# One pool of eight slots for the mixer's and FFN's short-lived tiles, and transfers that the scheduler counts in one line

## The chip, the cores and the metric

The kernel runs on one core of a Trainium2 chip. The time is the device time of one launch in microseconds (us). The kernel before takes 4589.91 us, the median of three runs (4589.24 to 4595.37).

## The reference, cut to what matters

Thirty-two images of 96 channels and 56 x 56 pixels pass through two layers. The first is a convolution block with 576 inner channels. The second works on the 3136 pixels as tokens: a mixer that goes through a Fourier transform over the tokens, and a feed-forward part (FFN) whose numbers are rounded to small float formats.

```python
# layer 0: convolution block, per image
h = relu(bn1(einsum('oc,bchw->bohw', w1, x)))          # 96 -> 576
h = relu(bndw(depthwise_conv3x3(h, wdw)))
x = x + bn2(einsum('oc,bchw->bohw', w2, h))            # 576 -> 96
# layer 1: on tokens t [image, 3136, 96]
h = relu(bn1(einsum('bnc,hc->bnh', layernorm(t), w1)))  # 96 -> 192
X = fft(h, axis=1, norm='ortho')
xr = relu(X.real * rd - X.imag * idg + rb)
xi = relu(X.imag * rd + X.real * idg + ib)
t = t + bn2(einsum('bnh,ch->bnc', ifft(xr + 1j * xi, axis=1, norm='ortho').real, w2))
u = layernorm(t)
h = relu(qlinear(u, W1, b1))                            # 96 -> 384, rounded
t = t + qlinear(h, W2, b2)
# ... (batch norms have stored statistics; qlinear rounds inputs, sums and biases)
```

## The kernel before

The kernel is written as a list of steps. Each step has an engine, an estimated cost, the steps it comes after, the buffers that it takes and gives back, a rank (which of the ready steps is preferred), and `late`, the time from the end of its work until its result counts as there. While the program is built, `Plan.emit` plays these steps through with the estimated times and writes the instructions in the order that comes out. On the chip each engine then works through its own list in that order and waits on semaphores where a result isn't there. The guesses are used at no other place: a wrong one does not change the result, it changes the order.

```python
START = {"last": 9, "front": 7, "mid": 62, "back": 98}     # offsets of rank for the stages
PACE = {"last": 3.023, "front": 0.4, "mid": 0.54, "back": 0.45}
OFF = (-4.5, 0.5, 0.5, 8.0)
AT = (3.0, 0.5)

class Plan:
    LATE = {"PE": 0.3, "ACT": 0.18, "DVE": 0.15}
    def moved(self, now, moves):                # `late` of a transfer
        size, rate, extra = moves
        start = now + 1.4
        end = start + size / rate
        self.moving = [m for m in self.moving if m[1] > start - 20]
        wait = sum(max(0.0, min(end, b) - max(start, a)) for a, b in self.moving)
        self.moving.append((start, start + 1.3 * size / rate))
        return end + wait + extra - now
    def emit(self):
        # ... of the ready steps of an idle engine, in order of rank:
                    short = {b for b in s.take if self.free[b] < s.take.count(b)}
                    if short or wanted.intersection(s.take):
                        wanted |= short
                        passed.append(item)
                        continue
        # ... and, when it is taken:
                    late = self.moved(now, s.late) if isinstance(s.late, tuple) else s.late
                    heapq.heappush(events, (now + cost, count, engine, None))
                    heapq.heappush(events, (now + cost + late, count + 1, None, s))

def read(n):    return n * 4, 170e3, 1.5        # a load: bytes, bytes per us, extra us
def written(n): return n * 4, 170e3, 3.0        # a write to memory
```

Four stages make an image. In the convolution, `unit` works on half an image and 128 of the inner channels. ACT makes a product of one tap in a tile of its own, and a transfer from GpSimd's queue adds it into `acc`; then ACT applies the ReLU to `acc`.

```python
nc.scalar.activation(acc[img, s, k], u["hs"][...], AF.Identity, scale=..., bias=...)        # line 643
nc.scalar.activation(u["p", dr][...], u["hs"][...], AF.Copy, scale=weight(dr, 0))          # line 659
nc.vector.scalar_tensor_tensor(dst, src, weight(dr, dc), dst, ALU.mult, ALU.add)           # line 670
nc.gpsimd.dma_start(out=t[...], in_=u["p", dr][...], accum_op=ALU.add)                     # line 678
nc.scalar.activation(acc[img, s, k], acc[img, s, k], AF.Relu)                              # line 687
# ... the transfer's step, with W = 28 * 56:
t = step("POOL", 1.0, add(None, 0), [t] + c, [], ["product"], late=(W * 128 * 4, 200e3, 0.0), rank=4 * n + 3)
```

`front` projects to 96 channels, keeps the tokens in memory (`tdr`), takes the norm, and sends the first transform's result to memory (`ydr`). `mid` reads it back and has three parts per half image, each with a tile V, a tile eo and a tile sb:

```python
u["V", part] = w2.tile([128, G, 2, S], F32, name="V")                        # pool of 2
u["eo", part] = w1.tile([128, G, 2, S], F32, name="eo", bufs=3)              # pool of 3
to = u["b", part] = w1.tile([128, G, SK], F32, name="sb", tag="brief", bufs=3)   # pool of 3
# ... t = step("PE", cost, spread(part), need, ["ps", "V", "eo", "brief"], ...)
# ... t = step("DVE", 2 * dve(392, 0.1), fold(part), [t], [], ["V", "brief"])
# ... t0 = step("PE", ..., half_project, folds, ["ps", "ps"], ["eo"]), and project(t) gives the other eo
```

Lines 1135 and 1136 (ACT) and 1152 (DVE) work on V and sb, lines 1167 and 1170 (DVE) fold them into eo. The pool `brief` of three holds sb, and also xn (the scaled tokens, line 979), pj and gc (results of the projection and of the inverse transform, lines 1235 and 1263) and o (the output, line 1463). `back` reads the mixer's result from memory (`gdr`), takes the norm (line 837 its square root on ACT, line 853 the reciprocal on DVE), and computes the FFN (lines 1350 to 1463).

Of the kernel before, what the change touches and what calls it, by code (L numbers as in the profile page):

```python
# [32 lines left out]
F32 = mybir.dt.float32  # L33
# [8 lines left out]
C = 96  # L42
HD = 576
S = 56
# [3 lines left out]
SK = 2 * S  # L48
# [7 lines left out]
G = 7  # L56
# [72 lines left out]
PACE = {"last": 3.023, "front": 0.4, "mid": 0.54, "back": 0.45}  # L129
CHAIN = 0.6  # L130

SPARSE = 0.75
FILLER = 0.23
FIRST = 15.0
# [20 lines left out]
class Plan:  # L155
# [12 lines left out]
    def __init__(self, free):  # L168
        self.free = dict(free)
        self.steps = []  # L170
        self.now = self.pace = 0.0
        self.window, self.share, self.slow = 0, {}, False
        self.moving = []
        self.filler, self.recent = None, []

    def stretched(self, now, work):
# [22 lines left out]

    def moved(self, now, moves):  # L200

        size, rate, extra = moves
        start = now + 1.4
        end = start + size / rate
        self.moving = [m for m in self.moving if m[1] > start - 20]
        wait = sum(max(0.0, min(end, b) - max(start, a)) for a, b in self.moving)
        self.moving.append((start, start + 1.3 * size / rate))
        return end + wait + extra - now

    def job(self, now, pace):  # L210

# [2 lines left out]
    def step(self, engine, cost, emit, after=(), take=(), give=(), late=None, rank=None):  # L214
        late = self.LATE.get(engine, 0.1) if late is None else late
        if rank is None:
            rank = self.now
            self.now += self.pace
        s = Step(engine, cost, emit, list(after), list(take), list(give), late, rank, len(self.steps))
        self.steps.append(s)  # L220
        return s
# [62 lines left out]
def tile_kernel(ctx: ExitStack, tc: tile.TileContext, d: dict, out: bass.AP):  # L284
# [66 lines left out]
    hl = [cst([128, RP + 1, S], f"hl{s}") for s in range(2)]  # L351


    scratch = [w1.tile([128, G * SK], F32, name="eo", bufs=3) for _ in range(3)]
    scratch += [w2.tile([128, G * SK], F32, name="V") for _ in range(2)]
    scratch.append(w1.tile([SK, 2 * G * SK], F32, name="wb"))
    scratch += [w2.tile([SK, G * HA], F32, name="yb") for _ in range(2)]
    used = [0] * len(scratch)
# [170 lines left out]
    def ffn():  # L529
# [6 lines left out]
        for o, v, p, n in ((b1q, fb, 128, 3), (b2q, fc, C, 1)):  # L536
# [9 lines left out]
    plan = Plan(  # L546
        {
# [4 lines left out]
        }  # L552
    )
# [9 lines left out]
        return fixed + n / 960  # L563

    def read(n):
        return n * 4, 170e3, 1.5

    def written(n):
        return n * 4, 170e3, 3.0

    bands_set = [step("DVE", 1.2, bands(j), rank=2.0 + j) for j in range(2)]
    sets = []
    for n, (f, count) in enumerate(((second, 7), (attention, 6), (mixer, 21), (ffn, 4))):
        t = step("SP", 0.55 * count, fetch, sets[-1:], late=(150e3, 170e3, 1.5), rank=-20.0 + n)
        sets.append(step("DVE", 3.0, f, sets[-1:] + [t], rank=14.0 + 4 * n))
    second_set, mixer_set, *mid_set = sets

# [22 lines left out]
    def unit(img, s, k):  # L600
# [96 lines left out]
            last = q == rest[-1]  # L697
            t = step("DVE", dve(W - 28, 0.16), tap(*q), [t] + c * last, [], ["hs"] * last, rank=4 * n + OFF[2] + at * 3.5 / len(rest))
        if k in DOUBLE:
            c = [step("POOL", 1.0, add(0, -up), c, [], ["product"], late=(W * 128 * 4, 200e3, 0.0), rank=4 * n + AT[1])]  # L700
        t = step("POOL", 1.0, add(None, 0), [t] + c, [], ["product"], late=(W * 128 * 4, 200e3, 0.0), rank=4 * n + 3)
        ready[img, s, k] = step("ACT", act(W, 0, 0.09), finish, [t], rank=4 * n + OFF[3])

    def last_channels(img, s):
# [265 lines left out]
    def mixer_in(img, s, j, v, after):  # L970
# [4 lines left out]
        def scale():  # L975

            at = slice(G * j, G * j + G)
            u["xn"] = w1.tile([SK, G, C], F32, name="xn", tag="brief", bufs=3)
            nc.vector.tensor_mul(u["xn"], v["t"][:, at, :], v["r"][:, at].unsqueeze(2).to_broadcast([SK, G, C]))

        t = step("DVE", dve(G * C, 0.06), scale, after + [sent[img, s]] * j + [mixer_set], ["brief"], ["norma", "xt"] * j)
# [90 lines left out]
    def mid(img, half):  # L1072
# [36 lines left out]
        def spread(part):  # L1109


            def f():
                u["V", part] = w2.tile([128, G, 2, S], F32, name="V")
                u["eo", part] = w1.tile([128, G, 2, S], F32, name="eo", bufs=3)
                u["X", part] = psum()
                pv = slots(u["X", part])
                for q in range(G):
                    for s in range(2) if part == 2 else (part,):
                        if part == 2:
                            o, lhsT = pv[64 * s : 64 * s + 64, q, 0:SK], u["yb", s][:, q, 128:HA]  # L1120
                        else:
                            o, lhsT = pv[:, q, 0:SK], u["yb", s][:, q, 0:128]
                        nc.tensor.matmul(o, lhsT=lhsT, rhs=u["wb"][:, G * s + q, :], start=True, stop=True)  # L1123

            return f
# [18 lines left out]
        def combine(part, op):  # L1144
            def f():
                rd = cw[:, part // 2, 0:1]
                X = slots(u["X", part])[:, 0:G, 0:SK]
                V = u["V", part].rearrange("p q r w -> p q (r w)")
                to = V
                if op == ALU.subtract:  # L1150
                    to = u["b", part] = w1.tile([128, G, SK], F32, name="sb", tag="brief", bufs=3)
                nc.vector.scalar_tensor_tensor(to, X, rd, V, ALU.mult, op)  # L1152

            return f
# [29 lines left out]
        for part in (0, 2, 1):  # L1184
            r = real and part != 1
            need = [w] + (yb if part == 2 else [yb[part]])
            cost = pe(SK, 128, 2 * G)
            t = step(
                "PE",
                cost,  # L1190
                spread(part),
                need,
                ["ps", "V", "eo", "brief"],
                ([YB] if part == 2 else []) + ([YB, WB] if part == 1 else []),
            )
            t = step("ACT", 2 * act(392, 2) + 0.24 * r, weigh(part), [t])
            t = step("DVE", dve(784), combine(part, ALU.subtract), [t])
            t = step("DVE", dve(784), combine(part, ALU.add), [t], [], ["ps"])
            t = step("ACT", act(784, 0, 0.09), bend(part), [t])
            t = step("DVE", 2 * dve(392, 0.1), fold(part), [t], [], ["V", "brief"])  # L1200
            folds.append(step("DVE", 0.08, place(part), [t]) if r else t)

        def half_project():
# [27 lines left out]

        def projected(t):
            def f():
                u["p", t] = w1.tile([SK, G * C], F32, name="pj", tag="brief", bufs=3)
                nc.scalar.activation(
                    u["p", t].rearrange("p (q c) -> p q c", c=C), slots(u["P", t])[0:SK, 0:G, 0:C], AF.Copy
                )

            return f
# [16 lines left out]
        def inverted(t):  # L1256
            def f():
                if (img, "g") not in sent:

                    gdr[img] = dram.tile([NP, SK, C], F32, name="gdr", bufs=3)  # L1260
                    sent[img, "g"] = True
                u["g", t] = w1.tile([SK, G * C], F32, name="gc", tag="brief", bufs=3)
                nc.scalar.activation(
                    u["g", t].rearrange("p (j w) -> p j w", j=2), u["I", t][0:SK, :, 0:n], AF.Copy
                )

            return f
# [9 lines left out]
            return f  # L1277

        turns.setdefault(img, [])
        t0 = step("PE", pe(C, SK, 2 * G) + 0.1, half_project, folds, ["ps", "ps"], ["eo"])  # L1280
        for t in range(2):
            p = step("PE", pe(C, SK, 2 * G), project(t), [t0], ["brief"], ["eo"])
            p = step("ACT", act(G * C), projected(t), [p], [], ["ps"])
            take = ["ps", "brief"] + ["gdr"] * (half == 0 and t == 0)
            p = step("PE", pe(n, SK, 4), invert(t), [p] + turns[img], take, ["brief"])
            turns[img] = [p]
            p = step("ACT", act(G * C), inverted(t), [p], [], ["ps"])
            sent[img, "g", half, t] = step("SP", 0.2, send(t), [p], [], ["brief"], late=written(SK * G * C))


    def back(img, h):
# [148 lines left out]
            nc.vector.tensor_scalar_add(u["y"], u["y"], b2q)  # L1440

        def total():
            u["o"] = w1.tile([C, G, SK], F32, name="o", tag="brief", bufs=3)
            u["ps"] = psum()
            pv = slots(u["ps"])
            for q in range(G):
                nc.tensor.matmul(
                    pv[0:C, q, 0:SK],
                    lhsT=u["t"][:, q, :],
                    rhs=ident[0:SK, 0:SK],  # L1450
                    start=(q in (0, 4)),
                    stop=False,
                    is_transpose=True,
                    skip_group_check=True,
                )
            yv = u["y"].rearrange("p (q w) -> p q w", w=SK)
            for a, b in HALVES:
                nc.tensor.matmul(
                    pv[0:C, a:b, 0:SK], lhsT=ident16, rhs=yv[:, a:b, :], start=False, stop=True, skip_group_check=True
                )  # L1460
# [98 lines left out]
```

## Time and profile before

| | us |
|---|---|
| time, median of 3 | 4589.91 |
| span of the profiled execution | 4584.2 |
| PE matmul busy | 4405.4 |
| VectorE (DVE) busy | 4330.6 |
| ScalarE (ACT) busy | 4114.5 |
| accumulations into acc: issue to landing, median of 256 | 8.0 |
| accumulations into another product: the same, median of 128 | 10.1 |

The profile is that of one execution. A busy share near 100% doesn't say that an engine bounds the kernel: [...] a filler matmul (line 1491) is put in wherever the plan sees PE idle for long. The lists of waits give, for an engine and a line, the line that it waited for, then the total, the times and the longest. A wait that several semaphores could have caused is put down to the one that came last. A timeline gives start, duration, engine, line, operation, and in brackets the idle time before it with what ended it.

### The profile page before, as it was taken

The page shows a single profiled execution, that of the slowest core. Times are in us where ns is not written, and L with a number is a line of the kernel's source. Part 1 is how long each engine was busy: PE and PEld are TensorE (multiplying, and loading weights), DVE is VectorE, ACT ScalarE, POOL GpSimd, SP SyncE. Part 2 cuts the span into 40 slices and gives each one's busy share as a digit, 9 for nine tenths or more (in the row PEclk, how much of TensorE's full clock was granted, in tenths as well). Part 3 has the DMA queues.
Part 4 walks back from the last instruction along what each step waited for, and adds up shares of the span by engine and source line. Part 5 has one row for each costly group of instructions (what it writes and reads, how often), then busy time and mean ns, then how long its engine had stood idle before and what let it go on. Part 6 is the DMA issues. An engine that isn't in the chain of part 4 may idle for free.

```text
span 4584.2 us, 88412 instructions
## 1 busy us (share of the span) xinstructions
PE 4405.4 (96%) x35128; PEld 3296.1 (72%) x35128; DVE 4330.6 (94%) x7053; ACT 4114.5 (90%) x5390; POOL 340.7 (7%) x403
## 2 busy tenths in 40 slices
PE   8989999999999999999999999999999999999998
PEld 5667776777777777777777777777777777777777
DVE  8998999999999999999999999999999999999967
ACT  5677999999999999999999999999999999999965
POOL 1000000000000000000000000000000000000000
PEclk9999999999999999999999999999999999999999
DMA  4666777767767777767777767777767777767663
GB/s 104 135 155 157 190 171 176 187 162 185 181 163 188 174 179 185 184 166 191 173 176 185 183 163 188 174 176 183 187 162 188 174 174 190 179 165 191 168 170 107
DMA packets 390993, 789.44 MB, mean 172 GB/s; under 512 B 135696, under 2 KB 236628, under 8 KB 390580
## 3 DMA queue, kind: packets, MB, share of 16 engines
q1 hardware_dynamic: 335028, 479.15, 36.2%
q0 software_dynamic: 55488, 304.64, 34.4%
q8 instruction: 276, 4.52, 0.4%
q14 instruction: 137, 1.12, 0.1%
q10 hardware_dynamic: 64, 0.01, 0.0%
HBM read 286.38 MB, written 192.68 MB: 105 GB/s over the span
## 4 chain that ended last, share of the span: by engine, by line
PE 48%; ACT 22%; DVE 16%; DMA 8%; issue 4%; POOLq 0%; ACTq 0%; POOL 0%; SPq 0%; DVEq 0%
PE pw L883 11%; DVE acc L670 10%; PE ps L617 9%; DMA acc<-product 7%; PE ps L1005 4%; PE ps L1123 4%; PE ps L755 3%; PE ps L1036 3%; ACT product L659 3%; ACT hs L627 2%; ACT acc L687 2%; ACT acc L643 2%; PE ps L1329 2%; ACT h L1410 2%; ACT h L1395 2%
## 5 line engine op out<-in xcount | busy, mean ns | idle before, releaser
L670 DVE SCALAR_TENSOR_TENSOR acc<-hs,wdw,acc 128x1540 f32<-128x1540 f32 (+2 forms) x1664 | 2970.3, 1792 | 26.6 <-ACT acc L643 20.8
L617 PE MATMUL ps<-xs,w1T 96*128 96x406 f32 x2048 | 819.8, 523 | 24.6 <-ACT h L1395 16.7
L883 PEld LDWEIGHTS pw<-w2T,acc 128*112 128x112 f32 x7168 | 754.3, 178 | 62.1 <-issue 36.4
L883 PE MATMUL pw<-w2T,acc 128*112 128x96 f32 x7168 | 790.8, 264 | 4.5 <-ACT acc L687 4.5
L659 ACT ACTIVATE product<-hs,wdw 128x1568 f32<-128x1568 f32 (+1 forms) x384 | 613.8, 1599 | 21.6 <-DMA product<-product 20.9
L617 PEld LDWEIGHTS ps<-xs,w1T 96*128 96x128 f32 x2048 | 368.2, 194 | 261.7 <-issue 174.0
L627 ACT ACTIVATE hs<-ps,b 128x812 f32<-128x812 f32 x512 | 481.5, 941 | 51.2 <-PE ps L617 46.8
L687 ACT ACTIVATE acc<-acc 128x1568 f32<-128x1568 f32 x256 | 387.5, 1514 | 90.9 <-DMA acc<-product 85.1
L678 POOL DMA_DIRECT2D acc<-product x256 | 222.7, 870 | 3193.9 <-DVE mf L859 781.6
L643 ACT ACTIVATE acc<-hs,bd,wdw 128x1568 f32<-128x1568 f32 x256 | 437.0, 1707 | 0.3
L755 PE MATMUL ps<-hl,band 128*64 128x385 f32 (+3 forms) x3072 | 416.1, 495 | 0.3 <-ACT hs L627 0.3
L1005 PE MATMUL ps<-watt,xnT 97*120 97x192 f32 x1792 | 345.3, 337 | 60.9 <-DVE V L1152 59.6
L1005 PEld LDWEIGHTS ps<-watt,xnT 97*120 97x120 f32 x1792 | 299.0, 187 | 125.3 <-DVE V L1152 65.6
L1123 PEld LDWEIGHTS ps<-wb,yb 112*128 112x128 f32 x3528 | 297.3, 164 | 66.5 <-issue 20.9
L1395 ACT ACTIVATE h<-ps 128x784 f16<-128x784 f32 x384 | 319.6, 835 | 25.8 <-PE ps L1383 22.0
L1350 ACT ACTIVATE u<-tt,mf,rf 112x96 fp8e5<-112x96 f32 x812 | 312.3, 460 | 16.6 <-DVE mf L859 16.5
L1123 PE MATMUL ps<-wb,yb 112*128 112x112 f32 x3528 | 321.8, 271 | 4.4 <-ACT hs L627 2.6
L1410 ACT ACTIVATE h<-h 128x784 fp8e5<-128x784 f16 x348 | 301.9, 867 | 14.9 <-DVE h L1401 14.8
L755 PEld LDWEIGHTS ps<-hl,band 128*64 128x64 f32 (+1 forms) x3072 | 151.9, 134 | 198.9 <-issue 164.2
L1152 DVE SCALAR_TENSOR_TENSOR sb<-ps,cw,V 128x784 f32<-128x784 f32 x192 | 197.0, 1026 | 31.1 <-ACT V L1136 25.4
L1018 ACT ACTIVATE z<-ps 120x768 f32<-120x768 f32 (+1 forms) x256 | 182.3, 725 | 44.9 <-PE ps L1005 44.9
L1036 PE MATMUL ps<-z,wa 56*64 56x384 f32 (+1 forms) x2048 | 217.5, 496 | 0.3
(171 smaller groups left out, 6663.3 us busy)
## 6 DMA issues: line engine op xcount, KB each, us to landing
acc<-product POOLq DMA_DIRECT2D x256, 784.0 KB, 8.0
product<-product POOLq DMA_DIRECT2D x128, 756.0 KB, 10.1
yb<-ydr SPq DMA_DIRECT2D x252, 294.0 KB
wd<-in_wd_dram SPq DMA_DIRECT2D x128, 349.1 KB
wb<-in_wb_dram SPq DMA_DIRECT2D x63, 686.0 KB
ydr<-ya SPq DMA_DIRECT2D x256, 168.0 KB
xs<-in_x_dram SPq DMA_DIRECT2D x64, 609.0 KB
tdr<-xt SPq DMA_DIRECT2D x64, 588.0 KB
```

Source lines behind the costliest of these rows:

```text
L617: nc.tensor.matmul(u[h][:, j, 0:QW], lhsT=w1T[:, 128 * k : 128 * (k + 1)], rhs=xs[img, s][0:C, at : at + QW], start=True, stop=True,)
L627: nc.scalar.activation(flat[:, 2 * h * QW : 2 * (h + 1) * QW].rearrange("p (j w) -> p j w", j=2), u[h][:, :, 0:QW], AF.Relu, bias=b1[:, k ...
L643: nc.scalar.activation(acc[img, s, k], u["hs"][:, o + up : o + up + R, :], AF.Identity, scale=weight(up, 0), bias=bd[:, k : k + 1],)
L659: nc.scalar.activation(u["p", dr][:, ra:rb, :], u["hs"][:, ra + o + dr : rb + o + dr, :], AF.Copy, scale=weight(dr, 0))
L670: nc.vector.scalar_tensor_tensor(dst, src, weight(dr, dc), dst, ALU.mult, ALU.add)
L687: nc.scalar.activation(acc[img, s, k], acc[img, s, k], AF.Relu)
L755: nc.tensor.matmul(pv[:, :, ca:cb], lhsT=band[rows, j, dc + 1, 64 * o : 64 * o + 64], rhs=H[rows, q : q + 7, ca + dc : cb + dc], skip_grou ...
L883: nc.tensor.matmul(u["pw"][0:SK, t, n % 4, 0:C], lhsT=src[rows, (G * t + n) * SK : (G * t + n + 1) * SK], rhs=rhs, skip_group_check=True, **k,
L1005: nc.tensor.matmul(pv[0:PK, q - a, 0:HA], lhsT=xnT[:, q, 0:PK], rhs=watt, start=True, stop=True,)
L1123: nc.tensor.matmul(o, lhsT=lhsT, rhs=u["wb"][:, G * s + q, :], start=True, stop=True)
L1395: nc.scalar.activation(u["h", c].rearrange("p (j w) -> p j w", j=2), u["H", c][:, :, 0:n], AF.Copy)
L1410: nc.scalar.activation(u["h8"][:, c, :], u["h", c], AF.Copy, saturate=False)
```

## The change

The tiles V and eo go into the pool `brief`, which grows from three slots to eight; 2 + 3 + 3 slots become 8 of the same size, so that any of the three kinds may have more than its share for a while. And the scheduler no longer gives each transfer its own rate with an addition for overlapping ones: all transfers stand in one line that drains at 225,000 bytes per us, with an extra of 0.5 us for loads and writes and of 1.3 us for accumulations.

```diff
+RATE = 225e3
+HARD = 0.5
+SOFT = 1.3
...
-        self.moving = []
+        self.moving = 0.0
...
-        size, rate, extra = moves
-        start = now + 1.4
-        end = start + size / rate
-        self.moving = [m for m in self.moving if m[1] > start - 20]
-        wait = sum(max(0.0, min(end, b) - max(start, a)) for a, b in self.moving)
-        self.moving.append((start, start + 1.3 * size / rate))
-        return end + wait + extra - now
+        size, extra = moves
+        self.moving = max(self.moving, now + 1.0) + size / RATE
+        return self.moving + extra - now
...
-            "xt": 1, "norma": 2, "brief": 3, "xnT": 1, "z": 2, "ya": 1, "wb": 1, "yb": 2,
-            "V": 2, "eo": 3, "real": 1, "wd": 1, "gd": 1, "tt": 2, "normf": 2, "u8": 1, "uT": 1,
+            "xt": 1, "norma": 2, "brief": 8, "xnT": 1, "z": 2, "ya": 1, "wb": 1, "yb": 2,
+            "real": 1, "wd": 1, "gd": 1, "tt": 2, "normf": 2, "u8": 1, "uT": 1,
...
     def read(n):
-        return n * 4, 170e3, 1.5
+        return n * 4, HARD
     def written(n):
-        return n * 4, 170e3, 3.0
+        return n * 4, HARD
...
-        t = step("POOL", 1.0, add(None, 0), [t] + c, [], ["product"], late=(W * 128 * 4, 200e3, 0.0), rank=4 * n + 3)
+        t = step("POOL", 1.0, add(None, 0), [t] + c, [], ["product"], late=(W * 128 * 4, SOFT), rank=4 * n + 3)
...
-                u["V", part] = w2.tile([128, G, 2, S], F32, name="V")
-                u["eo", part] = w1.tile([128, G, 2, S], F32, name="eo", bufs=3)
+                u["V", part] = w1.tile([128, G, 2, S], F32, name="V", tag="brief", bufs=8)
+                u["eo", part] = w1.tile([128, G, 2, S], F32, name="eo", tag="brief", bufs=8)
...
-                ["ps", "V", "eo", "brief"],
+                ["ps", "brief", "brief", "brief"],
```

The lines cut away change the same names in the same way: `bufs=3` becomes `bufs=8` for xn, sb, pj, gc and o, and every step that gave back V or eo gives back a `brief`.

More of the change, by code (lines that the diff above doesn't have):

```diff
@@ L351, in tile_kernel @@
     hl = [cst([128, RP + 1, S], f"hl{s}") for s in range(2)]
-    scratch = [w1.tile([128, G * SK], F32, name="eo", bufs=3) for _ in range(3)]
-    scratch += [w2.tile([128, G * SK], F32, name="V") for _ in range(2)]
+    scratch = [w1.tile([128, G * SK], F32, name="eo", tag="brief", bufs=8) for _ in range(3)]
+    scratch += [w1.tile([128, G * SK], F32, name="V", tag="brief", bufs=8) for _ in range(2)]
     scratch.append(w1.tile([SK, 2 * G * SK], F32, name="wb"))
@@ L573, in tile_kernel @@
     for n, (f, count) in enumerate(((second, 7), (attention, 6), (mixer, 21), (ffn, 4))):
-        t = step("SP", 0.55 * count, fetch, sets[-1:], late=(150e3, 170e3, 1.5), rank=-20.0 + n)
+        t = step("SP", 0.55 * count, fetch, sets[-1:], late=(150e3, HARD), rank=-20.0 + n)
         sets.append(step("DVE", 3.0, f, sets[-1:] + [t], rank=14.0 + 4 * n))
@@ L699, in unit @@
         if k in DOUBLE:
-            c = [step("POOL", 1.0, add(0, -up), c, [], ["product"], late=(W * 128 * 4, 200e3, 0.0), rank=4 * n + AT[1])]
-        t = step("POOL", 1.0, add(None, 0), [t] + c, [], ["product"], late=(W * 128 * 4, 200e3, 0.0), rank=4 * n + 3)
+            c = [step("POOL", 1.0, add(0, -up), c, [], ["product"], late=(W * 128 * 4, SOFT), rank=4 * n + AT[1])]
+        t = step("POOL", 1.0, add(None, 0), [t] + c, [], ["product"], late=(W * 128 * 4, SOFT), rank=4 * n + 3)
         ready[img, s, k] = step("ACT", act(W, 0, 0.09), finish, [t], rank=4 * n + OFF[3])
@@ L977, in scale @@
             at = slice(G * j, G * j + G)
-            u["xn"] = w1.tile([SK, G, C], F32, name="xn", tag="brief", bufs=3)
+            u["xn"] = w1.tile([SK, G, C], F32, name="xn", tag="brief", bufs=8)
             nc.vector.tensor_mul(u["xn"], v["t"][:, at, :], v["r"][:, at].unsqueeze(2).to_broadcast([SK, G, C]))
@@ L1150, in f @@
                 if op == ALU.subtract:
-                    to = u["b", part] = w1.tile([128, G, SK], F32, name="sb", tag="brief", bufs=3)
+                    to = u["b", part] = w1.tile([128, G, SK], F32, name="sb", tag="brief", bufs=8)
                 nc.vector.scalar_tensor_tensor(to, X, rd, V, ALU.mult, op)
@@ L1199, in mid @@
             t = step("ACT", act(784, 0, 0.09), bend(part), [t])
-            t = step("DVE", 2 * dve(392, 0.1), fold(part), [t], [], ["V", "brief"])
+            t = step("DVE", 2 * dve(392, 0.1), fold(part), [t], [], ["brief", "brief"])
             folds.append(step("DVE", 0.08, place(part), [t]) if r else t)
@@ L1233, in f @@
             def f():
-                u["p", t] = w1.tile([SK, G * C], F32, name="pj", tag="brief", bufs=3)
+                u["p", t] = w1.tile([SK, G * C], F32, name="pj", tag="brief", bufs=8)
                 nc.scalar.activation(
@@ L1261, in f @@
                     sent[img, "g"] = True
-                u["g", t] = w1.tile([SK, G * C], F32, name="gc", tag="brief", bufs=3)
+                u["g", t] = w1.tile([SK, G * C], F32, name="gc", tag="brief", bufs=8)
                 nc.scalar.activation(
@@ L1279, in mid @@
         turns.setdefault(img, [])
-        t0 = step("PE", pe(C, SK, 2 * G) + 0.1, half_project, folds, ["ps", "ps"], ["eo"])
+        t0 = step("PE", pe(C, SK, 2 * G) + 0.1, half_project, folds, ["ps", "ps"], ["brief"])
         for t in range(2):
-            p = step("PE", pe(C, SK, 2 * G), project(t), [t0], ["brief"], ["eo"])
+            p = step("PE", pe(C, SK, 2 * G), project(t), [t0], ["brief"], ["brief"])
             p = step("ACT", act(G * C), projected(t), [p], [], ["ps"])
@@ L1442, in total @@
         def total():
-            u["o"] = w1.tile([C, G, SK], F32, name="o", tag="brief", bufs=3)
+            u["o"] = w1.tile([C, G, SK], F32, name="o", tag="brief", bufs=8)
             u["ps"] = psum()
```

## The prediction

> **What bounds the kernel now.** I read the page first: the busy shares, the forty slices, the chain that ended last. Then the windows by stage, the waits of each engine in the steady part, and the timeline of one image.
>
> ```profile
> PE 4405.4 (96%) x35128; PEld 3296.1 (72%) x35128; DVE 4330.6 (94%) x7053; ACT 4114.5 (90%) x5390; POOL 340.7 (7%) x403
> ...
> PE 48%; ACT 22%; DVE 16%; DMA 8%; issue 4%; POOLq 0%; ACTq 0%; POOL 0%; SPq 0%; DVEq 0%
> ```
>
> Three engines are nearly full at once. PE's 96% holds matmuls that only keep its clock up (the row of line 1491: 710 in the steady part, 118.2 us), so PE has a little to give; DVE has no such filling. The chain passes through the accumulating transfers for about 8% of the span.
>
> ```profile
> 2026.64:2164.24 137.60, 133.82 (x1070) 99.41 (x1070) 132.43 (x215) 130.00 (x172) 10.46 (x12) 0.99 0.73 178
> 2164.24:2302.62 138.38, 135.30 (x1083) 100.51 (x1082) 133.88 (x215) 130.14 (x173) 10.46 (x12) 0.99 0.74 178
> ```
>
> Two images in a row; the columns are length, then busy time of PE, PEld, DVE, ACT, POOL, then clock, DMA share and GB/s. One image takes about 138 us and DVE works about 133 of it. The steady part, 230 to 4300 us, holds 4070/138 = 29.5 images. There DVE is busy 3907.0 us of 4070.0, so 163 us (4.0%) is all that any better order can win there.
>
> ```profile
> DVE rf L853 <- ACT sdf L837: 53.2, 55, 3.1
> DVE sb L1152 <- ACT V L1136: 23.4, 56, 0.9
> DVE y L1440 <- ACT y L1437: 19.3, 27, 0.7
> DVE acc L670 <- ACT acc L643: 17.0, 30, 2.2
> ...
> ACT acc L687 <- DMA acc<-product: 78.5, 36, 5.1
> ```
>
> Waits of DVE and of ACT, 230 to 4300 us: total, times, longest. DVE waits only for ACT, about once an image at each place: the order repeats from image to image, so a place that waits is paid nearly 30 times. ACT's largest wait is for a transfer. No wait of DVE or PE there ends on a load; in this part the loads hide.
>
> ```profile
> 2026.64 1.51 ACT L687 ACTIVATE acc<-acc 128x1568 f32<-128x1568 f32 x1 [1.93 <-DMA acc<-product]
> 2028.05 0.19 ACT L837 ACTIVATE sdf<-wf 112x7 f32<-112x7 f32 x1
> ...
> 2028.28 0.20 DVE L853 RECIPROCAL rf<-sdf 112x7 f32<-112x7 f32 x1 [1.25 <-ACT sdf L837]
> ...
> 2033.42 0.48 DVE L1440 TENSOR_SCALAR y<-y,b2q 96x784 f16<-96x784 f16 x1 [0.71 <-ACT y L1437]
> ```
>
> This joins the two lists. ACT stands 1.93 us at line 687 because the accumulation into acc has not landed. The square root queued behind it is late, so DVE stands 1.25 us, and about 5 us later another 0.71. One late transfer thus costs DVE 1.25 + 0.71 = 1.96 us an image.
>
> **What the Trainium skill says.** "DMA: Bandwidth & Descriptors", section "Issuing engines are not separate DMA queues": transfers of all queues run on the same 16 engines and interleave. Section "Queues, rings and completion order": an engine takes turns between the rows that have work. That is sharing, not one line. The trace agrees: an accumulation issued at 2017.10 us, with a second at 2018.20 and writes from 2018.55, was still awaited at 2026.6, 9.5 us on; the fastest of all took 5.6. "Perfetto Trace Analysis", section "Optimization Strategy": the same gap repeating on the engine that should be saturated can mean that buffers ran out. Here the repeating gaps of DVE end on ACT work, not on a release of V, eo or a brief tile, so the trace does not show this for the pool that grows.
>
> **The change part by part.**
>
> *Instructions.* None is added or taken away: the same tiles, sizes and engines. Memory is the same too: 2 V, 3 eo and 3 brief tiles, each up to 784 words a partition, become 8 slots. Only the order of emission, the slots and the semaphores differ. The sum of busy times stays, but for the fillers, so the price lies wholly in waits.
>
> *The pool.* Each part of the mixer takes a V, an eo and a brief tile, six parts an image. I estimate holding times from the timeline: V and sb each about 18 us, eo about 35 until its projection, and some 100 us an image for xn, pj, gc and o together. Then V is used 6*18 = 108 of 2*138 tile-us (39%), eo 210 of 414 (51%), brief 108 + 100 = 208 of 414 (50%); pooled, 526 of 1104 (48%). None was full, so pooling helps only in bursts. Three parts in flight still don't fit (9 tiles against 8). Each part must now find three tiles of one pool, beside xn, pj, gc and o. I give it -4 us.
>
> *The transfers.* The plan's guess of an accumulation of 802816 bytes standing alone, the POOL step's own 1.0 us included, was 1.0 + 1.4 + 4.01 = 6.41 us. It becomes 1.0 + 1.0 + 802816/225000 + 1.3 = 6.87. The trace gives 5.6 / 9.3 / 17.4 as least, median and longest of all accumulations. The plan's lengthening for company was the overlap with transfers already moving; now it is the backlog of one line. By the table of issues some 740 MB go into that line; at 225 GB/s that is 3290 of 4584 us, 72%. A line filled to 72% with pieces of about 2.6 us makes a newcomer wait about 0.72/(2*0.28)*2.6 = 3.3 us, so about 10 us against the median of 9.3. The old rule, by the same kind of estimate, came to about 9. The averages hardly differ; what improves is that a backlog cannot be counted away.
>
> At the costly place, however, the line is no better. With the load of wd (357 KB, issued at 2016.00) before it, it says 2018.7 + 3.57 + 1.3 + 1.0 = 2024.6 us for the transfer that landed at 2026.6; the old rule said about 2025.1. Both miss that a later transfer slows an earlier one. A plain load or write of 301056 bytes becomes 0.1 + 1.0 + 1.34 + 0.5 = 2.9 us, where a load was 4.8 and a write 6.3. The write of gdr whose second half was issued at 2023.15 landed only at 2031.66, 8.5 us later, so writes get optimistic. In the steady part that is cheap: gd and wd are loaded right after the product before (2052.5, 2085.3, 2120.6 us) and wanted about 33 us later.
>
> *Sum.* The DMA-linked loss of DVE is 1.96 us x 28 = 55 us. I expect the new order to keep about half, since the average guess is right and the case of a later competitor is not: -27. Pool: -4. Start and end, where tiles of an idle mixer serve the output (DVE waits 58 us at the end): -3. Optimistic writes and loads, seen as new waits: +12. The rest of DVE's waits, 153 - 55 = 98 us, are dealt anew by another order with no reason for a sign: 0, uncertain by about 30. The sum is -22, so 4590 - 22 = 4568; as the start numbers and rank offsets were left as they stood for the old guesses, I state 4570.
>
> **The rivals.**
>
> *The shaken order.* The plan is a greedy list whose result repeats every image: 1 us more of DVE wait an image is 30 us. START, PACE, OFF and AT are unchanged, so if they had been fitted to the old guesses, any other order is likely worse. For it: the sharp repetition of the waits. Against it: the lost 5 us an image show that no fit was perfect. It would give 4600 to 4640.
>
> *A new wait on a transfer.* With 0.5 us in place of 3.0 behind a write, the plan frees a slot early. xn or sb (DVE), or gc, pj, o (ACT), may then be sent to a slot whose last reader, a write to memory, is still going, and the bound engine stands. For it: 8.5 us measured against about 3. Against it: eight slots make the oldest free one old. Cost: 1 to 2 us an image, 4600 to 4650.
>
> *The whole DMA link goes.* If the line places line 687 late enough, all 55 us go and ACT gains its 78.5 us: about 4520. Against it stands the worked case above.
>
> *Nothing moves.* The wait turns up at another place of the image with the same sum: 4580 to 4595.
>
> **Range and chances.** The largest gain in sight is the 163 us of steady slack, of which 55 have a cause that the change touches. The largest loss is a wait or two of 1 to 2 us at a place paid 30 times. So 4525 to 4625 should hold it 8 times in 10. Faster by over 2% means below 4498, more than the whole DMA link and more again: 0.03. Slower by over 2% means above 4682, three fresh waits an image: 0.04. Within 2%: 0.93.
>
> **What would show it.** Counts and mean durations as before, DVE near 4330 us busy. ACT's waits for acc<-product fall from 85.1 us over the run to 30-60; if they vanish, the line was a better guess than I hold; if they grow, the rival is right. DVE's wait for sdf falls from 55.4 us to about 30. If "DMA" turns up as a releaser for lines 979 or 1152, or for ACT at 1235, 1263 or 1463, the early slot was the trap. If the matmuls of line 1329 wait for gd, the loads were. Unchanged DMA waits with a time off by over 20 us would mean that the redealt order decides, and my sum has its weight in the wrong term.

## The result, and the profile after

The changed kernel takes 4472.77 us (median of 4 runs, 4470.88 to 4477.12) against 4589.57 us beside it: 0.9747 of the time, 95% interval 0.973 to 0.9764. That is 117 us less, where 20 were predicted and 65 were the most that the range allowed.

The page of the kernel after, busy shares and the shares of the chain that ended last:

```profile
PE 4366.5 (98%) x34916; PEld 3248.3 (73%) x34916; DVE 4307.1 (96%) x7053; ACT 4103.5 (92%) x5390; POOL 339.6 (8%) x403
...
PE 37%; DVE 32%; ACT 15%; issue 3%; DMA 3%; ACTq 0%; DVEq 0%; POOLq 0%; SPq 0%
```

DVE and ACT execute as many instructions as before, PE 212 fewer, all of them fillers. The transfers' share of the chain falls from 8% to 3%, and DVE's rises from 16% to 32%; PE still holds the largest part.

Two images in a row in the windows of the kernel after (length, busy time of PE, PEld, DVE, ACT, POOL, then clock, DMA share, GB/s):

```profile
2061.38:2196.25 134.87, 133.18 (x1072) 98.45 (x1072) 132.45 (x214) 129.41 (x173) 10.40 (x12) 1.00 0.75 182
2196.25:2331.10 134.85, 133.27 (x1073) 98.54 (x1073) 132.44 (x215) 129.60 (x173) 10.41 (x12) 1.00 0.75 183
```

An image takes 134.9 us where it took 138.0 (the mean of 137.60 and 138.38 in the two windows of before). Times 29.5 images of the steady part that is some 91 of the 117 us, and the rest must lie at the start and the end.

Waits of DVE, then of ACT, in the kernel after from 230 to 4200 us (total, times, longest):

```profile
DVE h L1401 <- ACT h L1395: 60.3, 84, 1.2
DVE eo L1167 <- ACT V L1158: 6.7, 7, 2.1
DVE ra L853 <- ACT sda L837: 5.0, 3, 4.3
DVE rf L853 <- ACT sdf L837: 3.6, 4, 2.3
DVE sta L827 <- ACT xt L933: 1.5, 1, 1.5
DVE sb L1152 <- ACT V L1136: 0.6, 1, 0.6
DVE y L1440 <- ACT y L1437: 0.3, 1, 0.3
...
ACT acc L687 <- DMA acc<-product: 12.5, 6, 3.9
```

ACT's wait for an accumulation at line 687, 78.5 us before, is 12.5. The waits of DVE for the square root, for V, for y and for acc, some 113 us before, come to about 5. One wait is new in size: line 1401 (FFN) for ACT, 60.3 us, where it was 15.1. In one image the timeline of DVE shows only that:

```profile
2061.38 0.42 DVE L1401 TENSOR_SCALAR h<-h,b1q 128x784 f16<-128x784 f16 x1 [1.24 <-ACT h L1395]
2096.89 0.42 DVE L1401 TENSOR_SCALAR h<-h,b1q 128x784 f16<-128x784 f16 x1 [0.19 <-ACT h L1395]
2128.57 0.42 DVE L1401 TENSOR_SCALAR h<-h,b1q 128x784 f16<-128x784 f16 x1 [0.71 <-ACT h L1395]
```

That is 2.1 us an image, where the kernel before lost about 5. The transfers themselves are no faster. The last line of the view of line 678, the kernel after:

```profile
DMA to landing us min/median/max: 5.6/9.5/15.1
```

The median was 9.3. So the shorter waits do not come from transfers that land sooner; the instructions stand later in the order, where the result is there.

### The profile page after: what moved, and what is told of

It is laid out like the page before. It is cut to its first block, busy times and chain, and to the rows that moved or that the text cites. A ratio compares the mean times of both kernels' runs of the same rounds, so it can differ in the third digit from the quotient of the medians.

```text
span 4469.5 us, 87997 instructions
## 1 busy us (share of the span) xinstructions
PE 4366.5 (98%) x34916; PEld 3248.3 (73%) x34916; DVE 4307.1 (96%) x7053; ACT 4103.5 (92%) x5390; POOL 339.6 (8%) x403
## 4 chain that ended last, share of the span: by engine, by line
PE 37%; DVE 32%; ACT 15%; issue 3%; DMA 3%; ACTq 0%; DVEq 0%; POOLq 0%; SPq 0%
DVE acc L670 20%; PE pw L883 10%; PE ps L617 5%; PE ps L1005 3%; PE ps L1036 3%; PE ps L1123 3%; PE ps L1329 2%; ACT h L1395 2%; DVE sb L1152 2%; DVE V L1152 2%; DMA acc<-product 2%; ACT product L659 1%; ACT hs L627 1%; PE ps L755 1%; PE ps L1447 1%
## 5 line engine op out<-in xcount | busy, mean ns | idle before, releaser
L617 PE MATMUL ps<-xs,w1T 96*128 96x406 f32 x2048 | 808.9, 517 | 27.2 <-ACT al L784 12.9
L617 PEld LDWEIGHTS ps<-xs,w1T 96*128 96x128 f32 x2048 | 355.6, 190 | 291.5 <-issue 165.1
L687 ACT ACTIVATE acc<-acc 128x1568 f32<-128x1568 f32 x256 | 388.0, 1516 | 26.1 <-DMA acc<-product 19.9
L1401 DVE TENSOR_SCALAR h<-h,b1q 128x784 f16<-128x784 f16 x384 | 162.3, 423 | 88.9 <-ACT h L1395 88.8
L1329 PE MATMUL ps<-gd,wd 114*112 114x96 f32 x1792 | 200.2, 264 | 2.3 <-DMA gd<-gdr 2.0
```

The costliest lines, as they stand in the source:

```text
L617: nc.tensor.matmul(u[h][:, j, 0:QW], lhsT=w1T[:, 128 * k : 128 * (k + 1)], rhs=xs[img, s][0:C, at : at + QW], start=True, stop=True,)
```

## The experiments

Three theories were on record. A: the better guess of the transfers lets engines find their inputs where the order puts them; the pool is worth little. B: the pool pays. C: any other order could have come out so; that of before was unlucky.

Beside the times I use two numbers from the plan, the reckoning that fixes the order. Its own end is what the plan believes the kernel takes. Its *late share* is the share of accumulations that landed over 2 us later after their issue than the plan had reckoned, by the trace (the first and last 20 left out). These numbers are no hardware times; they show how far the order is built on what happens.

```
kernel                       plan's end  measured  beyond  late share  ACT waits for acc<-product
before                         4488.7     4589.6    101      12%        85.1
after                          4465.9     4472.8      7       2%        19.9
E1 line only                   4474.0     4486.8     13       1%        26.9
E2 pool only                   4483.4     4597.5    114      15%        77.3
E3 before, nudged              4487.3     4642.7    155      22%       109.5
E4 after, nudged               4469.8     4520.6     51       8%        46.8
E7 before, +2.0 us             4509.1     4550.4     41       0%         5.6
E8 after, no line              4511.1     4681.8    171      12%        54.8
E10 after, own line            4494.0     4574.7     81       6%        79.8
E11 after, HARD 3.0            4499.7     4495.7     -4       2%        24.9
E12 after, SOFT 3.0            4469.3     4476.6      7       0%         9.3
```

**E1 and E2: one part at a time.** E1 takes from the change only the line:

```diff
-        size, rate, extra = moves
-        # ... overlaps with the transfers that move
+        size, extra = moves
+        self.moving = max(self.moving, now + 1.0) + size / RATE
+        return self.moving + extra - now
```

> The pools of before (V 2, eo 3, brief 3), the transfers in one line as after. Theory A (the better guess of transfers lets the engines find their inputs where the order puts them; the pool is worth little): 4475 to 4500 us, ACT's waits for acc<-product near 20-30 us, DVE's waits for sdf below 15 us. Theory B (the pool of eight is what pays): 4570 to 4600 us, waits as before. Theory C (any other order could have come out so; the order of before was unlucky): anywhere from 4480 to 4590 us, without a tie to the waits for transfers.

E2 takes only the pool:

```diff
-            "brief": 3, ... "V": 2, "eo": 3,
+            "brief": 8, ...
-                ["ps", "V", "eo", "brief"],
+                ["ps", "brief", "brief", "brief"],
```

> One pool of eight as after, the old guesses of transfers. Theory A: 4570 to 4590 us, ACT's waits for acc<-product 70 us or more. Theory B: 4475 to 4500 us. Theory C: anywhere from 4480 to 4590 us.

E1: 4486.76 us, 0.9764 of before (0.9748 to 0.9781). E2: 4597.53 us, 1.0007 (0.9999 to 1.0016). B falls: the pool alone gives nothing. With the line there, the kernel with the pool is 14 us faster than the one without (4472.8 against 4486.8); the next two runs show that a difference of this size can come from the order alone, so this is not shown to be the pool's. E2's waits, of ACT and then of DVE, over the whole run:

```profile
ACT acc L687 <- DMA acc<-product: 77.3, 38, 4.0
...
DVE rf L853 <- ACT sdf L837: 57.1, 60, 2.5
```

The wait for accumulations and the late square root stay with the old guesses and go with them: in E1 they are 26.9 and 3.0 us.

**E3 and E4: how much is luck.** Both kernels with one unrelated number moved by a hair:

```diff
-START = {"last": 9, "front": 7, "mid": 62, "back": 98}
+START = {"last": 9, "front": 7, "mid": 62, "back": 97.9}
```

> The kernel before with one number that has nothing to do with either part moved by a hair: START of back 98 to 97.9. A and B: another order of the same kind, 4575 to 4605 us. C: a jump by 30 us or more to either side.

> The kernel after with the same nudge, START of back 98 to 97.9. A: 4465 to 4485 us. C: a jump by 30 us or more, most likely up.

4642.71 us (1.0101 of before, 1.0086 to 1.0116) and 4520.57 us. Both lose about 48 us, so both expectations of A fail: an order is worth that much by itself, and a difference of 1% between two orders says nothing of the rule that made them. But the gap between the two nudged kernels is 122 us, like the 117 without the nudge. Three pairs with the same pool or the same nudge give the change of guess 106 (before to E1), 125 (E2 to after) and, with the pool, 122 us. C explains the scatter within each kind and not the gap. Only this one nudge was tried. What it did shows in the same wait: in E3, ACT's waits for accumulations grew from 85.1 to 109.5 us, its longest.

```profile
ACT acc L687 <- DMA acc<-product: 109.5, 64, 5.9
```

**E5, E6 and E9: the same order, accumulations that land sooner.** To see what late accumulations cost, order and guesses stay and each accumulating transfer moves only its first 14 rows (of 27 or 28). The other rows are left unadded, and some 150 MB less are moved, so these times are not those of the full computation.

```diff
                 ra, rb, _, _ = span(dr, 0)
                 t = acc[img, s, k] if to is None else u["p", to]
+                rb = ra + R // 2
```

> The kernel before, order and guesses untouched, but each accumulating transfer moves only the first 14 of its rows, so that it lands some 3 us or more sooner; the other rows are left unadded, and the memory traffic is some 150 MB less. Theory A (late accumulations, spread from ACT to DVE and PE, are the whole difference between the time and the plan): 4480 to 4500 us, no wait of ACT for acc<-product in the steady part. If something else in the order of before is slow (C, or other wrong estimates): 4540 us or more.

> The kernel after with the same cut of the accumulating transfers. A: it had little left to lose, 4455 to 4470 us. If most of the gain lay elsewhere, after would gain from this as much as before does, some 50 us or more.

> The nudged kernel before (START of back 97.9) with the accumulating transfers cut to the first 14 rows; the other rows are left unadded. A (the nudge cost 49 us because its order runs into more late accumulations): 4475 to 4495 us, as the cut kernel before. If the nudge cost something else: 4520 us or more.

The kernel before falls by 110.6 us, from 4593.1 to 4482.57 us (0.9757, 0.9734 to 0.9781), 6 us under its plan's end. The kernel after falls by 16, to 4456.50. The nudged kernel before falls by 136, to 4506.43; that is more than A wanted left, 19 us above its plan, and what these 19 are wasn't tried. The whole run before, DVE's five longest waits, then the longest of ACT and of PE:

```profile
DVE rf L853 <- ACT sdf L837: 55.4, 62, 3.1
DVE h L1401 <- ACT h L1395: 44.5, 37, 6.4
DVE sb L1152 <- ACT V L1136: 25.4, 59, 1.1
DVE y L1440 <- ACT y L1437: 24.8, 31, 1.8
DVE acc L670 <- ACT acc L643: 20.8, 32, 2.3
ACT acc L687 <- DMA acc<-product: 85.1, 40, 5.1
PE ps L1005 <- DVE V L1152: 59.6, 29, 2.1
```

The same waits in E5 (line numbers from 678 on are one higher here):

```profile
DVE h L1402 <- ACT h L1396: 30.9, 14, 6.4
DVE sb L1153 <- ACT V L1137: 24.4, 59, 1.1
DVE rf L854 <- ACT sdf L838: 13.8, 35, 0.8
...
DVE y L1441 <- ACT y L1438: 8.5, 9, 2.7
DVE acc L670 <- ACT acc L643: 8.5, 31, 0.4
ACT acc L688 <- DMA acc<-product: 9.3, 9, 2.5
PE ps L1006 <- DVE V L1153: 22.2, 28, 1.6
```

Together with ACT's wait for accumulations, and in an untouched order, DVE's waits for the square root, y, acc and h fell, and PE's at line 1005. Only the wait for V stays. So the late accumulation reached DVE at four places and PE at one, and not only at the two of DVE that I had followed. The transfers as a whole got shorter too, so contention goes down with the lateness; but in the steady part of before, PE, DVE and ACT had waited on other transfers for no more than 6.2 us in total.

PE's wait at line 1005 cost more than its own length. One image of before without and one with a drop of the clock, then the drop by itself (clock third from the end):

```profile
1837.30:1974.30 137.00, 133.21 (x1082) 98.99 (x1076) 133.12 (x215) 129.85 (x174) 10.48 (x12) 1.00 0.74 180
1974.30:2112.60 138.30, 134.52 (x1078) 100.10 (x1074) 133.13 (x215) 130.00 (x174) 10.47 (x12) 0.99 0.74 178
2041.10:2044.50 3.40, 3.40 (x18) 2.56 (x17) 3.40 (x5) 3.40 (x5) 0.00 (x0) 0.50 0.00 0
```

In 13 of the 28 images between 455 and 4319 us (an image reaches from one instruction of line 687 to the same one of the next image) the granted TensorE clock fell to half for 3.4 or 6.8 us, each time within 2 us of that wait's end (2039.37 us here, after 2.14 us of waiting). These 13 images took 139.2 us on average, the other 15 took 136.9. In the kernel after, where the wait is 0.8 us at most, and in E5, 27 of 28 images have no drop; they take 134.7 and 134.9 us. So some 1.0 of the 3.2 us that an image gained, about 27 us in all, goes with the drops; how much of that is the half clock and how much the waits around it, no run separates.

**E7 and E8: is the average of the guess what counts?** E7 keeps the old rule and adds 2.0 us to each accumulation; E8 takes the line out of the new rule and puts its average in:

```diff
-        ... late=(W * 128 * 4, 200e3, 0.0)          # E7, from before
+        ... late=(W * 128 * 4, 200e3, 2.0)
-        self.moving = max(self.moving, now + 1.0) + size / RATE     # E8, from after
-        return self.moving + extra - now
+        return 1.0 + size / RATE + extra + 3.0
```

> The kernel before with 2.0 us more in the plan's guess of each accumulation, the old rule of overlaps kept. If the average of the guess is what was wrong: 4500 to 4530 us. If the scatter of the guess is what was wrong (the old rule forgets a backlog): 4550 us or more.

> The kernel after without the line: each transfer is guessed as if alone, plus a fixed 3.0 us, which is about the line's average wait. If the average is what matters: 4500 to 4530 us. If the line (who waits behind whom) is what matters: 4560 us or more.

E7: 4550.36 us (0.9905, 0.9877 to 0.9933). E8: 4681.81 us (1.0187, 1.0155 to 1.0219), the slowest of all, though its average guess, 9.87 us against 8.67 measured, was on the safe side. A fixed guess knows nothing of who stands in front: the spread (standard deviation) of measured less guessed was 2.20 us, against 1.45 before and 1.02 after. So a good average does not bring the gain. That the spread of the accumulations is what makes E8 slow is not shown: its late share is that of before, ACT waits less for them (54.8 us), and its guesses of loads and writes changed too. E7, just inside the range given for the scatter, shows the other side. With 2 us more on every accumulation, late ones vanish, but the plan must hold work back (its end rises by 20 us), and other waits come up, DVE's and then PE's:

```profile
DVE tt L1334 <- PE ps L1329: 37.9, 61, 1.7
...
PE pw L1491 <- ACT xt L933: 34.2, 44, 1.1
```

They were 5.8 and 0.9 us. The second is a filler matmul that waits in PE's queue for the tile pw; why this order meets it 44 times stays open.

**E10: what must stand in the line.** Only accumulations queue, with 2.0 us more each so that the average stays; loads and writes are guessed as if alone plus 3.0 us:

```diff
+        if extra == HARD:
+            return 1.0 + size / RATE + extra + 3.0
         self.moving = max(self.moving, now + 1.0) + size / RATE
-        return self.moving + extra - now
+        return self.moving + extra + 2.0 - now
```

> The kernel after, but only accumulations stand in the line, with 2.0 us more each so that the average guess stays near 9.5 us; loads and writes are guessed as if alone plus 3.0 us. If accumulations wait for each other only, the guess stays good: 4495 to 4515 us. If loads and writes in front of them are what the guess has to know: 4550 us or more.

4574.72 us (0.9962, 0.9948 to 0.9975). That is 102 us above the kernel after, twice what the nudge moves: most of the gain needs the loads and writes in the same line. In this order too, the wait for accumulations is ACT's longest, 79.8 us.

**The rules on the same traces.** Each rule can also be fed with the issue times and sizes of a trace and compared with the landings of all 384 accumulations there. Standard deviation of measured less guessed, in us, and in brackets the share that landed over 2 us late:

```
rule                                     trace of before   trace of after
one constant                             2.37              2.19
accumulations alone in a line            1.87              1.70
old rule (overlaps)                      1.67 (23%)        1.45 (19%)
one line at 225 GB/s (the change)        1.21 (5%)         1.06 (2%)
two queues that share 240 GB/s           1.11 (3%)         1.06 (3%)
```

The line is right to about 1 us, and two queues that share, which is nearer to what the Trainium skill says ("DMA: Bandwidth & Descriptors", section "Queues, rings and completion order"), are hardly better.

**E11 and E12: the two extras.**

```diff
-HARD = 0.5          # E11
+HARD = 3.0
-SOFT = 1.3          # E12
+SOFT = 3.0
```

> The kernel after with HARD 3.0 in place of 0.5, so that loads and writes are held to arrive 2.5 us later; accumulations are guessed as after. If the short extra of loads and writes is a false promise that after pays for: 4475 us or less. If it costs nothing because such results are wanted much later: 4495 to 4520 us, by the plan's less free order alone.

> The kernel after with SOFT 3.0 in place of 1.3: each accumulation is held to land 1.7 us later, the line kept; a try for a faster version, since the kernel after still lost some 16 us to late accumulations. If more caution is all that is left to win: 4460 to 4470 us, ACT's waits for acc<-product below 10 us. If caution costs the plan as much as it saves, or the other order brings other waits: 4473 to 4500 us.

E11: 4495.65 us (0.979, 0.9775 to 0.9804), 23 us above the kernel after. The plan's own end rises by 34, and ACT's wait for accumulations does not fall (24.9 us), so holding loads and writes back bought nothing here; but the nudge alone moved more than 23 us. E12: 4476.62 us (0.9758, 0.9739 to 0.9778), no different from the kernel after, though ACT's wait for accumulations fell from 19.9 to 9.3 us. DVE's waits changed places: at line 1401 they fell from 88.8 to 65.0 us over the whole run, and one of 1.2 us grew to 22.6:

```profile
DVE h L1401 <- ACT h L1395: 65.0, 68, 6.4
DVE sb L1152 <- ACT real L1140: 22.6, 27, 1.2
```

No full computation here was faster than the kernel after.

## Why the prediction was wrong, point by point

- **The bound.** Right for the steady part: DVE's busy time per image hardly moved (132.4 and 133.9 us before, 132.4 after), and its idle time there fell from 163 us to 83. The other 26 us of the gain came at the start and the end, where the sum had -3.
- **"The DMA-linked loss of DVE is 1.96 us x 28 = 55 us."** This term failed first. With accumulations landing sooner in the same order (E5) 111 us went, twice that. I followed one late transfer down the timeline to two waits of DVE and stopped; those at acc and h, and PE's at line 1005 with the clock drops behind it, were not in the sum. It went on. My reading, not tested by itself, is that an engine that is 1.9 us behind in a fixed order is behind for all that follows until it has slack, and ACT at 90% has little.
- **"I expect the new order to keep about half."** The step that failed most. E6 puts what was left in the kernel after at 16 us against 111, so the term that I set at -27 came to about -94. I had compared averages (about 9 and 10 us; the plans say 8.8 and 9.9) and found them alike, which was right, and the conclusion was wrong: what changed was how many guesses missed. Over 2 us late were 12% before and 2% after, and E8 shows that a good average is not enough, at 4682 us. The estimate of the average was itself rough: the plan's transfers add up to 786 MB, not 740, with which the same formula gives about 11 us instead of 10.
- **The worked case.** One transfer, 2 us late under either rule because a later one slowed it, stood for all. That it landed after 9.5 us also does not tell sharing from a line, as either can delay it. Over 384 transfers the effect of sharing is small: the sharing rule gains at most 0.1 us of spread over the line. A distribution was wanted, not an example.
- **Pool, -4.** Alone it gave nothing (+4 us, within the runs' scatter); the 14 us beside the line are less than a nudge moves.
- **Optimistic loads and writes, +12.** It did not come. PE's waits for gd came to 2.0 us in all, and without the short extra the kernel was 23 us slower (E11), not faster.
- **The shaken order, 0 give or take 30.** Too small: a nudge of 0.1 in one rank moved both kernels by some 48 us. But it does not account for the gap between the two rules, 117 us without the nudge and 122 with it.
- **The rivals.** "The whole DMA link goes" was nearest to what happened (ACT's wait at line 687 fell from 85.1 to 19.9 us), and I had sized it at 4520 with the 55 us. No wait of DVE for a write still leaving a slot appeared.

In the plan's terms: the order got 23 us better by its own reckoning (4488.7 to 4465.9), and the chip's distance to it shrank from 101 us to 7. Those two make the 117; the second, 94, is close to what the cuts show, 111 less 16.

## What to carry to other kernels

Where the order of instructions is fixed from estimated times, compare each estimate with the trace as a distribution, and look at the share that comes late rather than at the mean; the cheapest model that remembers the backlog of all transfers was worth 2.4%. To size a wait that repeats, take away its cause in the same order and measure, since following it down one timeline found only half of its cost. And before a 1% difference between two schedules is put down to an idea, nudge something unrelated: here that alone moved the time by 1%.

## What was unexpected of the hardware

Transfers of two queues behaved, for this purpose, nearly like one line at 225 GB/s: landing times of 802816-byte accumulations, 5.6 to 17.4 us in the trace of before, were met with a spread of 1.21 us (1.06 in the trace of after), with loads and writes counted in. Cutting accumulations to about half their rows brought the average from 9.3 to 6.5 us, more than their own bytes would (802816/225000/2 = 1.8 us); that each also stood behind less would explain the rest. And DVE's busy time fell from 4330.6 to 4307.1 us with the same 7053 instructions, whose durations add up to more than before (4847.8 and 4874.9 us). The records of neighbouring instructions overlap, by 517.2 us in all before and 567.8 after, and busy time counts an overlap once, so even a busy sum shifts a little with the order.
